# Softmax sums over keys by strided VectorE sums through DRAM, in a two-layer graph network on one core

## The chip, the core and the metric

The kernel runs on one core of one Trainium2 chip. The metric is the device time of one execution in microseconds (us). Before the change the median of three runs is 2721.17 us (2719.03 to 2722.04).

A core has five engines that run side by side, each with its own queue of instructions, executed in order: TensorE (PE, matrix products), VectorE (DVE), ScalarE (ACT), GpSimd (POOL) and SyncE (SP). In this kernel nearly all DMA transfers are issued by SP; 16 DMA engines carry them out. An instruction waits until the semaphores it needs are set, and everything behind it on the same engine waits with it.

## The reference

The input x is 64 batches of 256 tokens with 512 features, and adj is a 256 x 256 matrix of zeros and ones. Everything is float32. Layer 0 is attention with 8 heads of 64 features, masked by adj; layer 1 is a graph attention layer with one head. Each has a residual connection and a layer norm.

```python
# layer 0
q, k, v = x @ Wq + bq, x @ Wk + bk, x @ Wv + bv          # split into 8 heads
scores = einsum('bqhd,bkhd->bhqk', q, k) / sqrt(64) + (1 - adj) * -1e9
attn = softmax(scores, axis=-1)                          # sums over keys k
out = einsum('bhqk,bkhd->bqhd', attn, v)
x = layernorm(x + out @ Wo + bo)
# layer 1
h = x @ W
e = leaky_relu((h @ a1)[:, :, None] + (h @ a2)[:, None, :], 0.2) * adj
att = softmax(e, axis=2)
x = layernorm(x + elu(einsum('bij,bjf->bif', att, h) + beta * h))
```

The change concerns the denominators of the first softmax: for every batch, head and query, the sum of the exponentials over the 256 keys.

## The kernel before, in words

The kernel works on pairs of batches: 32 pairs, `pair(m, ...)`, each with two batches, `batch(m, s, ...)` with s 0 and 1.

For a pair, x is brought in transposed (`xin`, `xT`), and three products give q, k (features on partitions) and v (tokens on partitions). Each large product is done in two-by-two blocks with seven block products in place of eight (`project`, line 437 in the profile, tiles `ps_chain`, `ps_cross`, `ps_second`, `ps_fourth`, `ps_pair`). That needs sums and differences of the blocks of both sides. For Wq and Wk they are made once and stored in DRAM; in every later pair the seven left sides are fetched again, one at a time, into a rotating set of buffers called `piece` (`streamed`, lines 385 and 390). For Wv, Wo and W they stay in SBUF (`weight_sums`).

Attention of one batch (`attention_by_keys`): for each of four pairs of heads, TensorE makes the scores with keys on partitions and queries along the row (`scores`, line 756, tile `ps_sc`); VectorE adds the mask (line 763); ACT takes the exponential (line 765, tile `pT`, 128 partitions by two blocks of keys by 256 queries); POOL adds the two blocks of keys, so that 128 partial sums are left for every head and query (line 768, tile `both`). Then `denominators` sums over the 128 partitions by multiplying with ones on TensorE (line 781, tile `ps_den`), VectorE takes the reciprocal (line 798, tile `inv`), ACT sums both for a check of the range (line 794, into `range_sb`), and SP writes the rows of `inv` to DRAM and reads them back spread over all partitions (lines 806 and 810, tile `inv_all`). The values are mixed on TensorE without the denominators (`mixed`, line 733, tile `ps_pv`), copied out (line 831) and multiplied with `inv_all` by VectorE (line 836, tile `oT`). The product with Wo follows (`o`). The last batch takes its sums directly from `pT` and spreads the reciprocals with TensorE.

Layer 1 of a batch: two dot products with `wa_sb` (line 937), a row that is turned through DRAM (lines 960 to 963, tile `row`), `z` on VectorE (line 966), the leaky ReLU, mask, maximum, exponential and scale (lines 972 to 986, tile `e`), a transposition through DRAM (lines 1003 to 1010, `square`, `att_b`, `attT`), the product with x (`spread`, tile `yT`), the product with W (`u`), and the finish (lines 697 to 704).

The order of all instructions is fixed before the program is built. Every operation is entered in a `Plan` with its engine and an assumed duration. On TensorE the order is given by turns: `take_turn` sorts by round (the pair's number plus `LATER`) and, within a round, by the list `ROUND`; `FINISH` can give the operations of the last pairs an order of their own, and the last `OPEN` operations of TensorE may be placed in any order. `place` then lays the operations of all engines out in time with these durations, a lag between engines (`LAG`; for SP it stands for the transfer) and the numbers of buffers (`slots`), and what comes out is the order in every queue. Nothing of it is decided at run time.

## Time and profile before

| | |
|---|---|
| median of three runs | 2721.17 us |
| profiled execution | 2720.1 us |
| its span | 2718.3 us, granted TensorE clock 0.997 |
| TensorE busy | 2696.2 us, 99% |
| VectorE busy | 1956.4 us, 72% |
| ScalarE busy | 1548.9 us, 57% |
| GpSimd busy | 1721.8 us, 63% |
| DMA on SP's queue | 297.68 MB, 41.4% of 16 engines' span |

The profile comes from one execution. Its span runs from the first to the last instruction that the profiler saw; the execution's own time is 1.8 us longer. Busy time is the time in which an engine executed something, counted once where instructions overlap. Products of float32 show as two records each, so 8 of them show as 16. In the groups of instructions a row gives line, engine, operation, output and inputs, shapes and count; then the busy time, the mean time of one, the idle time of the engine before them and what ended it. For matrix products the mean of one is longer than what it occupies, since they overlap in a pipeline. In the list of waits a row gives who waited for whom, the total in us, the number of times and the longest.

### The profile page before, as it was taken

The page shows a single profiled execution, that of the slowest core. Times are in us where ns is not written, and L with a number is a line of the kernel's source. Part 1 is how long each engine was busy: PE and PEld are TensorE (multiplying, and loading weights), DVE is VectorE, ACT ScalarE, POOL GpSimd, SP SyncE. Part 2 cuts the span into 40 slices and gives each one's busy share as a digit, 9 for nine tenths or more (in the row PEclk, how much of TensorE's full clock was granted, in tenths as well). Part 3 has the DMA queues.
Part 4 walks back from the last instruction along what each step waited for, and adds up shares of the span by engine and source line. Part 5 has one row for each costly group of instructions (what it writes and reads, how often), then busy time and mean ns, then how long its engine had stood idle before and what let it go on. Part 6 is the DMA issues. An engine that isn't in the chain of part 4 may idle for free.

```text
span 2718.3 us, 47307 instructions
## 1 busy us (share of the span) xinstructions
PE 2696.2 (99%) x15919; PEld 2268.6 (83%) x15919; DVE 1956.4 (72%) x3677; ACT 1548.9 (57%) x3713; POOL 1721.8 (63%) x2254
## 2 busy tenths in 40 slices
PE   9999999999999999999999999999999999999997
PEld 7888888888888888888888888888888888888886
DVE  6777677777777677777767777777767777776766
ACT  3455556556556565565555655655656556555566
POOL 5756666665666656666666666566665666666654
PEclk9999999999999999999999999999999999999998
DMA  8434434344443444434443434444344443443221
GB/s 245 103 100 123 121 96 117 96 121 125 99 121 86 119 129 106 106 104 105 125 119 98 115 95 125 125 98 120 88 120 129 106 107 104 104 126 103 83 70 45
DMA packets 579056, 300.79 MB, mean 111 GB/s; under 512 B 404864, under 2 KB 509816, under 8 KB 578808
## 3 DMA queue, kind: packets, MB, share of 16 engines
q1 hardware_dynamic: 578680, 297.68, 41.4%
q8 instruction: 130, 2.13, 0.3%
q14 instruction: 118, 0.97, 0.1%
q0 software_dynamic: 128, 0.01, 0.0%
HBM read 245.11 MB, written 52.48 MB: 109 GB/s over the span
## 4 chain that ended last, share of the span: by engine, by line
PE 97%; DVE 1%; POOL 0%; ACT 0%; issue 0%; DMA 0%; SPq 0%; ACTq 0%; POOLq 0%; DVEq 0%
PE ps_chain L437 33%; PE ps_cross L437 22%; PE ps_pair L437 10%; PE ps_sc L756 8%; PE ps_pv L733 8%; PE ps_second L437 6%; PE ps_fourth L437 6%; PE ps_den L781 2%; DVE junk L543 0%; DMA xin<-in_x_dram 0%; ACT junk L569 0%; DMA row<-line 0%; SPq L631 0%; PE ps_y L1021 0%; PE ps_plain L502 0%
## 5 line engine op out<-in xcount | busy, mean ns | idle before, releaser
L768 POOL TENSOR_TENSOR both<-pT 128x256 f32<-128x256 f32 x504 | 354.6, 731 | 383.1 <-ACT pT L765 383.1
L763 DVE TENSOR_TENSOR pT<-ps_sc,maskT_sb 128x512 f32<-128x512 f32 x512 | 324.0, 680 | 85.4 <-PE ps_sc L756 85.4
L765 ACT ACTIVATE pT<-pT 128x512 f32<-128x512 f32 x512 | 304.0, 625 | 52.3 <-DVE pT L763 49.7
L937 DVE SCALAR_TENSOR_TENSOR junk<-x,wa_sb 128x512 f32<-128x512 f32 x256 | 206.8, 833 | 109.4 <-ACT x L586 108.2
L756 PE MATMUL ps_sc<-qT,kT 64*128 64x256 f32 x2048 | 238.4, 382 | 0.0
L733 PE MATMUL ps_pv<-pT,v 128*64 128x256 f32 x2048 | 235.1, 382 | 0.0
L756 PEld LDWEIGHTS ps_sc<-qT,kT 64*128 64x128 f32 x2048 | 192.8, 187 | 44.4 <-issue 24.6
L474 ACT COPY u<-ps_chain 128x256 f32<-128x256 f32 x126 | 46.9, 372 | 318.4 <-PE ps_chain L437 318.2
L586 ACT ACTIVATE x<-x,nmr,rs 128x512 f32<-128x512 f32 x256 | 197.5, 808 | 44.7 <-POOL nmr L582 44.6
L733 PEld LDWEIGHTS ps_pv<-pT,v 128*64 128x64 f32 x2048 | 141.4, 137 | 91.0 <-DVE kT L483 12.8
L1046 POOL TENSOR_TENSOR X_sums<-x 128x256 f32<-128x256 f32 x126 | 151.6, 1213 | 100.1 <-ACT x L586 98.6
L569 ACT ACTIVATE junk<-x,mean 128x512 f32<-128x512 f32 x256 | 182.2, 714 | 3.8 <-DVE mean L575 3.6
L569 ACT ACTIVATE junk<-x 128x512 f32<-128x512 f32 x256 | 159.4, 625 | 38.6 <-DVE x L914 31.8
L717 POOL TENSOR_TENSOR x<-x,res_sb 128x512 f32<-128x512 f32 x128 | 175.7, 1374 | 0.0
L580 POOL TENSOR_SCALAR rs<-sq 128x2 f32<-128x2 f32 (+1 forms) x130 | 34.8, 268 | 208.8 <-ACT junk L569 203.5
L408 POOL TENSOR_TENSOR oS<-oT 128x256 f32<-128x256 f32 x126 | 92.2, 731 | 86.7 <-DVE mean L575 53.0
L836 DVE TENSOR_TENSOR oT<-oT,inv_all 128x512 f32<-128x512 f32 x126 | 132.7, 1091 | 0.0
L975 POOL TENSOR_TENSOR e<-e,adj_sb 128x512 f32<-128x512 f32 (+1 forms) x66 | 82.2, 1247 | 77.0 <-DVE e L972 77.0
L437 PE MATMUL ps_chain<-so_sb,oS 128*128 128x256 f32 x504 | 129.3, 379 | 0.0
L437 PE MATMUL ps_chain<-sw_sb,yS 128*128 128x256 f32 x504 | 129.2, 379 | 0.0
L798 DVE RECIPROCAL inv<-ps_den 128x256 f32<-128x256 f32 x64 | 112.5, 1758 | 18.5 <-ACT junk L794 9.3
L408 POOL TENSOR_TENSOR yS<-yT 128x256 f32<-128x256 f32 x126 | 91.8, 729 | 51.7 <-DVE yT L483 31.8
(242 smaller groups left out, 7162.7 us busy)
## 6 DMA issues: line engine op xcount, KB each, us to landing
x<-in_x_dram SPq DMA_DIRECT2D x64, 512.0 KB
out_dram<-x SPq DMA_DIRECT2D x128, 256.0 KB
inv_all<-rows SPq DMA_DIRECT2D x126, 256.0 KB
xin<-in_x_dram SPq DMA_DIRECT2D x248, 128.0 KB
wq_sums<-wq_sums SPq DMA_DIRECT2D x124, 256.0 KB
wk_sums<-wk_sums SPq DMA_DIRECT2D x124, 256.0 KB
wq_sums<-in_L_gnn_Wq_dram SPq DMA_DIRECT2D x93, 256.0 KB
wk_sums<-in_L_gnn_Wk_dram SPq DMA_DIRECT2D x93, 256.0 KB
```

The source lines that it names most:

```text
L408: plan.op("POOL", 180 + 545 * width // P, lambda: nc.gpsimd.tensor_tensor(dst(), p(), m(), ALU.subtract), reads, writes)
L437: nc.tensor.matmul(dst[:, f, :], lhs, rhs, start=start and f == 0 and c == 0, stop=c == inner - 1, skip_group_check=True)
L569: plan.op("ACT", 700, lambda: nc.scalar.activation(junk[A], X[:, t, :], func, bias=mean[:, i:i + 1] if bias else 0.0, accum_out=to[:, i:i ...
L586: plan.op("ACT", 810, lambda i=i, t=t: nc.scalar.activation(X[:, t, :], X[:, t, :], AF.Identity, bias=nm[:, i:i + 1], scale=rs[:, i:i + 1] ...
L717: plan.op("POOL", 1270, lambda t=t: nc.gpsimd.tensor_tensor(X[:, t, :], X[:, t, :], res_sb[A], ALU.add), [res_sb], tokens(t))
L733: nc.tensor.matmul(acc[r * HD:(r + 1) * HD, i, :], V[:, 2 * k + s, h * HD:(h + 1) * HD], pT[h][:, k, :], start=k == 0, stop=k == NT - 1)
L756: nc.tensor.matmul(acc[j][:, k, :], kT[r:r + HD, c, key_blk(k)], own(qT, r, c), start=True, stop=True)
L763: plan.op("DVE", 690, lambda h=h, i=i: nc.vector.tensor_add(pT[h][A], acc[i][A], maskT_sb[A]), [acc[i], maskT_sb], [pT[h]])
L765: plan.op("ACT", 620, lambda h=h: nc.scalar.activation(pT[h][A], pT[h][A], AF.Exp, scale=1.0 / HD ** 0.5), [pT[h]], [pT[h]])
L768: plan.op("POOL", 725, lambda h=h, i=i: nc.gpsimd.tensor_tensor(both[c][:, i, :], pT[h][:, 0, :], pT[h][:, 1, :], ALU.add), [pT[h]], [(bot ...
L937: plan.op("DVE", 780, lambda t=t, i=i, junk=junk: nc.vector.scalar_tensor_tensor(junk[A], X[:, t, :], 1.0, wa_sb[:, i, :], op0=ALU.mult, o ...
L1046: plan.op("POOL", ns, lambda: nc.gpsimd.tensor_tensor(dst(), p(), m(), op), reads, writes)
```

## The change

The denominators of all batches but those of the last pair are no longer summed by TensorE. SP writes the four tiles `both` of a batch to DRAM (`keys`: 128 partial sums by 8 heads by 256 queries, 1 MB) and reads them back in four loads of another layout (`few`: in each group of 32 partitions, one partition holds 32 keys by 64 of the 2048 sums, in runs of 256 bytes). VectorE adds up the 32 keys in four strided sums (`part`). Four groups of keys are left; they go through DRAM once more (`parts`, `four`), and VectorE adds these and takes the reciprocal on 64 partitions by 32 columns (`den`). SP writes the reciprocals to `rows`, and the spread to `inv_all` is the same as before, now in a function of its own, `to_all`. The check of the range sums 32 columns on 64 partitions in place of 256 on 128; `range_sb` is set to one first. The last pair (`near`) takes its sums on TensorE directly from `pT`, as the last batch did before, in `denominators_near`.

With that go: the left sides of the product with Wv are streamed through `piece` like those of Wq and Wk, so that `wv_sb` and its sums no longer stay in SBUF, and there are seven `piece` buffers, not six; `z` is made by ACT, except in the last pair; `ROUND` has another order, `FINISH` is empty, `OPEN` is 60 and the lag of SP 5000 ns.

```diff
-ROUND = ("sums1", "mix1", "scores0", "spread1", "v", "u1", "attention0", "sums0", "mix0", "scores1", "o1", "x",
-         "logits1", "q", "spread0", "o0", "attention1", "u0", "k", "logits0")
+ROUND = ("sums1", "mix1", "scores0", "v", "spread1", "sums0", "mix0", "scores1", "attention0", "o1", "x", "k",
+         "logits1", "u1", "q", "spread0", "o0", "u0", "attention1", "logits0")
...
-FINISH = (("sums1", 1), ("mix1", 1), ("scores0", 0), ("v", 0), ("attention0", 1), ("spread1", 2), ("sums0", 0), ("u1",
...
+FINISH = ()
...
-    LAG = {"PE": 260.0, "DVE": 70.0, "ACT": 70.0, "POOL": 90.0, "SP": 4200.0}
+    LAG = {"PE": 260.0, "DVE": 70.0, "ACT": 70.0, "POOL": 90.0, "SP": 5000.0}
...
-    OPEN = 70
+    OPEN = 60
...
-    slots = {"xin": 2, "x": 4, "two": 6, "xP": 1, "piece": 6, "full": 4, "half": 18, "xS": 2, "st": 76, "ps": 8, "rows": 4, "svT": 4, "line": 4, "square": 4}
+    slots = {"xin": 2, "x": 4, "two": 6, "xP": 1, "piece": 7, "full": 4, "half": 18, "xS": 2, "st": 76, "ps": 8, "rows": 4, "svT": 4, "line": 4, "square": 4,
+             "keys": 3, "parts": 3, "few": 1, "part": 2, "four": 2, "den": 2}
...
-    wv_sb = weight(Wv, "wv_sb")
...
+    plan.op("POOL", 100, lambda: nc.gpsimd.memset(range_sb[A], 1.0), [], [range_sb])
...
-            wq_sb, wk_sb = sb("two", [C, D], "wq_sb"), sb("two", [C, D], "wk_sb")
+            wq_sb, wk_sb, wv_sb = (sb("two", [C, D], name) for name in ("wq_sb", "wk_sb", "wv_sb"))
...
+            load(wv_sb, Wv)
...
-            left["v"] = weight_sums(wv_sb, "sv_sb", "POOL")
+            lv, left["v"] = streamed(wv_sb, Wv, "wv_sums")
...
-        project(left["v"], right, False, [V], *gather(
-            lambda q: (lambda: V[:, 2 * q[1]:2 * q[1] + 2, half(q[0])], (V, q)), wide=True), width=N)
+        project(lv if m == 0 else left["v"], right, False, [V], *gather(
+            lambda q: (lambda: V[:, 2 * q[1]:2 * q[1] + 2, half(q[0])], (V, q)), wide=True), width=N, first=m == 0)
...
             def denominators():
+
+                keys, parts = Buf(dram_pool, "keys", [P, H * N], "keys"), Buf(dram_pool, "parts", [4, H * N], "parts")
+                for c in range(C):
+                    plan.op("SP", 500, lambda c=c: nc.sync.dma_start(
+                        keys[:, 2 * c * N:2 * (c + 1) * N], both[c][A].rearrange("p i n -> p (i n)")), [both[c]],
+                        [(keys, c)])
+
+                few, part = sb("few", [32, 64], "few"), sb("part", [64], "part")
+                for g in range(4):
+                    plan.op("SP", 800, lambda g=g: nc.sync.dma_start(
+                        few[32 * g:32 * g + 32], keys[32 * g:32 * g + 32, :].rearrange("k (c n) -> c k n", n=64)),
+                        [keys], [(few, g)])
+                for j in range(4):
+                    plan.op("DVE", 950, lambda at=slice(16 * j, 16 * j + 16): nc.vector.tensor_reduce(
+                        part[:, at], few[:, :, at].rearrange("p k n -> p n k"), AX.X, ALU.add), [few], [(part, j)])
+                plan.op("SP", 500, lambda: nc.sync.dma_start(
+                    parts[A].rearrange("g (c n) -> (g c) n", n=64), part[A]), [part], [parts])
+                four, den = sb("four", [4, 32], "four"), sb("den", [2, 32], "den")
+                plan.op("SP", 500, lambda: nc.sync.dma_start(
+                    four[0:HD], parts[A].rearrange("g (c n) -> c g n", n=32)), [parts], [four])
+                plan.op("DVE", 340, lambda: nc.vector.tensor_reduce(
+                    den[0:HD, 0, :], four[0:HD].rearrange("p g n -> p n g"), AX.X, ALU.add), [four], [(den, 0)])
+                plan.op("DVE", 280, lambda: nc.vector.reciprocal(den[0:HD, 1, :], den[0:HD, 0, :]), [(den, 0)],
+                        [(den, 1)])
+                for i in range(2):
+                    junk = sb("half", [32], "junk")
+                    plan.op("ACT", 400, lambda i=i, junk=junk: nc.scalar.activation(
+                        junk[0:HD], den[0:HD, i, :], AF.Identity, accum_out=range_sb[0:HD, i, b:b + 1]), [(den, i)],
+                        [junk, (range_sb, (i, b))])
+                plan.op("SP", 500, lambda: nc.sync.dma_start(
+                    rows[A].rearrange("h (c n) -> (h c) n", n=32), den[0:HD, 1, :]), [(den, 1)], [rows])
+                to_all()
+
+            def denominators_near():
                 turn("sums")
...
-                    for k in range(NT if last else 1):
+                    for k in range(NT):
...
-                                    pT[2 * c + i][:, k, :] if last else both[c][:, i, :],
...
-                if last:
-                    plan.op("PE", 1500, pe, pT, [acc], mode="sums", claims=[inv])
-                else:
-                    plan.op("PE", 1000, pe, both, [acc], mode="sums", claims=[inv])
...
+                plan.op("PE", 1860, pe, pT, [acc], mode="sums", claims=[inv])
                 plan.op("DVE", 1750, lambda: nc.vector.reciprocal(inv[A], acc[A]), [acc], [inv])
...
-            spread_inv = denominators()
+            spread_inv = denominators_near() if near else denominators()
...
         for t in range(NT):
-            plan.op("DVE", 480, lambda t=t: nc.vector.tensor_scalar(
-                z[:, t, :], row[A], sv[:, t, 1:2], None, ALU.add), [row, (sv, (0, t))], [(z, t)])
+            if near:
+                plan.op("DVE", 480, lambda t=t: nc.vector.tensor_scalar(
+                    z[:, t, :], row[A], sv[:, t, 1:2], None, ALU.add), [row, (sv, (0, t))], [(z, t)])
+            else:
+                plan.op("ACT", 440, lambda t=t: nc.scalar.activation(
+                    z[:, t, :], row[A], AF.Identity, bias=sv[:, t, 1:2]), [row, (sv, (0, t))], [(z, t)])
```

In both versions `both` is made for every batch whose sums do not come directly from `pT`: all but the last one before, all but the last two after.

## The prediction

> **What bounds the kernel now.** I read the page from the top: the span, the engines' busy time, then the chain that ended last, followed back from the last instruction.
>
> ```profile
> span 2718.3 us, 47307 instructions
> ...
> PE 2696.2 (99%) x15919; PEld 2268.6 (83%) x15919; DVE 1956.4 (72%) x3677; ACT 1548.9 (57%) x3713; POOL 1721.8 (63%) x2254
> ...
> PE 97%; DVE 1%; POOL 0%; ACT 0%; issue 0%; DMA 0%; SPq 0%; ACTq 0%; POOLq 0%; DVEq 0%
> ```
>
> TensorE is busy all the time and makes up 97% of the chain; no other engine reaches three quarters. Busy time by stretch (columns: stretch, its length, busy time of PE, PEld, DVE, ACT, POOL with instruction counts, granted clock, mean busy share of the 16 DMA engines, GB/s) shows one steady round of one pair of batches, then the start and the last pair:
>
> ```profile
> 1007.94:1091.58 83.64, 83.64 (x498) 70.61 (x498) 60.64 (x114) 48.27 (x116) 53.67 (x70) 1.00 0.44 111
> 8.00:90.00 82.00, 80.91 (x429) 67.95 (x428) 61.00 (x88) 30.78 (x68) 50.45 (x50) 1.00 0.81 222
> 2597.20:2718.30 121.10, 104.56 (x597) 83.88 (x597) 79.60 (x176) 72.68 (x175) 59.74 (x92) 0.94 0.19 56
> ```
>
> A round is 83.64 us with PE busy for all of it. DMA is light in the round (0.44) but heavy at the start (0.81). TensorE's own waits, the longest of them, are these; the first is the program's start, the next two lie in the last pair:
>
> ```profile
> PE tr_x L620 <- DMA xin<-in_x_dram: 4.3, 2, 3.7
> PE ps_chain L437 <- ACT attT L999: 1.5, 1, 1.5
> PE tr_a L996 <- DVE rc L983: 1.4, 1, 1.4
> ```
>
> So time taken off TensorE's queue counts in full, as long as nothing new makes it wait. The groups of the sums (busy, mean ns, then idle before) and one round's piece of TensorE's timeline (start, duration):
>
> ```profile
> L781 PE MATMUL ps_den<-both,ones 128*32 128x256 f32 x1008 | 67.5, 385 | 0.0
> L798 DVE RECIPROCAL inv<-ps_den 128x256 f32<-128x256 f32 x64 | 112.5, 1758 | 18.5 <-ACT junk L794 9.3 <-PE ps_den L781 9.2
> L966 DVE TENSOR_SCALAR z<-row,s 128x256 f32<-128x256 f32 x124 | 65.1, 566 | 6.9 <-DMA row<-line 6.4
> L977 DVE TENSOR_REDUCE nm<-e 128x2 f32<-128x512 f32 (+1 forms) x66 | 43.5, 659 | 2.0 <-POOL e L975 2.0
> ```
>
> ```profile
> 1085.09 1.89 PE L437 MATMUL ps_chain<-xS,wk_sums 128*128 128x256 f32 x8
> 1086.90 1.07 PE L781 MATMUL ps_den<-both,ones 128*32 128x256 f32 x16
> 1087.91 3.67 PE L733 MATMUL ps_pv<-pT,v 128*64 128x256 f32 x32
> ```
>
> The sums of one batch occupy 67.5/63 = 1.07 us of busy time, and 1.01 us from their start to the next group's start.
>
> [...]the store to square is issued at 1027.57 us and the reads that wait for it at 1029.66, 2.1 us. [...]The loads into few fill 32 partitions at a time, as those of att_b do[...]; the four sums step by 256 bytes, and no row of the kernel before shows such a step.
>
> **The change part by part**, against the profiled execution (2720.1 us, its span 2718.3; the median of the three timed runs is 2721.17, so 1.1 us above it).
>
> *Taken off TensorE.* 62 of 63 batches lose their ps_den group: 62 x 1.01 to 1.07 = 62.6 to 66.3 us. I take 64. Batch 62 goes from 8 to 16 products, which the last batch's group already shows (start to start 1.86 us against 1.01): +0.9.
>
> *VectorE, per batch.* Out: the reciprocal 1.76 and two z operations (2 x 0.53 = 1.05 by busy time): 2.8 us. In: four strided sums of 32 x 16 elements a partition. Nearest row L977, 128x512 in, 0.66 us contiguous; [...]I bound it above by double, 1.32; taken 1.0, so 4.0 (2.6 to 5.3). The two small operations on 64 partitions: I take 0.3 each. Net +1.8 (0.4 to 3.1), +3.6 a round: 60.6 + 3.6 = 64 of about 81.5 us, 79%. Free on the average; covered by TensorE's own work, and uncovered it would cost those 3.6 us a round, 112 over 31 rounds.
>
> *ACT.* z moves here: two 128x256 ACTIVATEs of about 0.44 (L794 0.41, L477 0.46), +0.9 per batch. The two range sums shrink from 256 columns to 32, between 0 and -0.8. At most +1.8 a round on 48.3. POOL: one memset more; its additions (L768, 0.73 us) stay.
>
> *SP's queue.* Before, 48 DMAs a pair: x 2, out 4, inv_all 4, xin 8, q and k pieces 14, square 2, att_b 8, line 2, row 2, rows 2. Added: keys 8, few 8, parts 2, four 2, v pieces 7: 75. Issue times from the trace (about 0.38 us for a plain one, 0.66 for one with 1024 pieces as xin, 0.6 for small ones): 8 x 0.38 + 8 x 0.66 + 4 x 0.6 + 7 x 0.36 = 13 us on some 24, 37 of 81.5. Room, but in order: while SP stands at few (waiting for keys to land) every piece and store behind it stands too.
>
> *DMA engines.* Prices from these stretches (same columns): the store to square with 256 KB, the four loads of att_b with 256 KB in 2048 packets, and a piece-rich stretch:
>
> ```profile
> 1028.00:1029.50 1.50, 1.50 (x9) 1.32 (x8) 0.67 (x2) 0.67 (x2) 1.42 (x2) 1.00 0.50 175
> 1030.50:1034.50 4.00, 4.00 (x34) 2.68 (x35) 1.52 (x4) 1.68 (x4) 3.31 (x3) 1.00 0.45 72
> 1050.50:1054.00 3.50, 3.50 (x18) 3.09 (x17) 2.11 (x4) 2.24 (x6) 2.92 (x4) 1.00 0.83 293
> ```
>
> Square: 0.50 x 1.5 = 0.75 us of all 16 engines, so keys (1 MB) 3.0 a batch. att_b: 0.45 x 4.0 = 1.8 us, 14 ns of one engine for each packet. few has 4096 packets of 256 bytes a batch: 3.6 us if a packet costs the same, 7.2 if a byte does; taken 5.4. Pieces: 0.83 x 3.5 = 2.9 us for 1.03 MB, 0.74 each, 5.2 for seven. A pair adds 6.0 + 10.8 + 5.2 + about 1 = 23 (19 to 27) to 0.44 x 83.64 = 36.8: 60 of 81.5 us, 73%. Hidden on the average.
>
> *The new chain of one batch.* After the last addition of both: keys 2.1, few about 7 (four issues, 5.4 of data[...]), sums 4, parts 2, four 2, small sums 1, rows 1.9 (issue at 1035.95, inv_all's at 1037.82), inv_all 3.7: 24 us. In the new order scores0 is followed by v 12.1, spread1 3.1, mix0 3.7, scores1 3.7, o1 6, k 12.1, u1 6, q 12.1, spread0 3.1, then o0 (durations of these groups in the trace): 62 us. The additions end 12.5 us after scores0 began (1007.9 to 1020.4), so about 25 us remain. sums1 is needed only in the next round's o1, later still. Not on the path.
>
> *v streamed.* With seven buffers the pieces of a product set can all be fetched before it begins; k and q follow each other with only u1's 6 us between, yet q's first piece may load as soon as k's first product is done, 18 us ahead. At the start four sums of Wv move from POOL to VectorE (wq_sums shows 1.64 us each, 6.6 in all, needed only behind scores0 at about 38 us), four stores of 256 KB are added, and the first keys and few fall where the DMA engines already run at 0.81: 82 x 0.81 = 66 us, plus about 20, is 86 of 82. I charge 4 us (0 to 12). If the engines had spare capacity there, it would be 0.
>
> *The end.* No order by FINISH, the last 60 TensorE operations free in place of 70, batch 62 without keys: the last pair's PE idle is 16.5 us; I charge +2 (-5 to +8).
>
> *Small waits.* DMA at 73% and VectorE at 79% will now and then be late: 0.15 us a round, 5 us (0 to 20).
>
> Sum: 2720.1 - 64 + 0.9 + 4 + 2 + 5 = **2668 us**, median taken the same. Its own range is 2650 to 2692.
>
> **Rivals.** *Partly eaten.* Pieces of q stand behind few and xin (1 MB, up to 3.2 us for one issue[...]), and each batch loses half to nine tenths of its microsecond: 2668 + 62 x (0.5 to 0.9) = 2699 to 2724, about 2705. For it: keys1, few1, xin and q's pieces all fall within k and u1. Against it: not one TensorE wait on a piece before.
>
> *VectorE stands at few: slower.* The four sums sit in order in VectorE's queue. If few lands late, behind them wait the additions that empty PSUM (L483, L914), and TensorE runs out of its eight PSUM buffers. The price is what TensorE stands per batch; it decides at 1.0 us, where the saving is gone. Assuming that few is 5 us late and that PSUM covers 3 of them, TensorE stands 2: 2668 + 124 = 2790. For it: order fixed beforehand, no slack in PE. Against it: the 25 us of slack let the sums be placed late, and VectorE stood only 6.4 us in 15 waits for row, its one regular DMA wait.
>
> *DMA becomes the bound.* few's packets would have to cost (83.6 - 36.8 - 12.2) x 16 / 8192 = 68 ns to cancel the gain, nearly five times att_b's. At 90 ns a round is 95 us, and the kernel near 3070. Only an effect of the 8 KB step between the rows of keys that att_b (1 KB step) doesn't show could do it.
>
> **How the numbers follow.** A change under 0.2% (5.4 us) can't be told from none. As forecast 0.58; partly eaten 0.14 (0.09 of it still faster, 0.05 no change); VectorE at few 0.20; DMA-bound 0.08. Faster 0.67, same 0.05, slower 0.28. The range 2648 to 2785 holds nearly all of the first two and half of the third, about 0.8.
>
> **What would show it.** Right: ps_den left in two batches only; a steady round of 81.5 us with PE busy throughout; DMA share near 0.73; the strided sums near 1.0 us each; PE still above 98%. Wrong: a round above 83.6 us; TensorE or VectorE waiting for few, wv_sums, wq_sums or wk_sums; DMA share near 1; a sum of 1.5 us or more; over 12 us lost before 100 us or after the last pair began.

## The result and the profile after

The changed kernel takes 2740.09 us (median of five runs, 2734.37 to 2744.66) against 2720.3 us before (median of five on the same chip, the three above among them): 1.0073 of it, 95% interval 1.0058 to 1.0089. It is 0.7% slower, where 1.9% faster was forecast. The profiled execution takes 2742.66 us, its span is 2740.9 us, 22.6 us more than before.

The page of the kernel after: span, busy times, SP's DMA queue (packets, MB, share of 16 engines), and the shares of the chain that ended last.

```profile
span 2740.9 us, 47862 instructions
...
PE 2662.1 (97%) x14943; PEld 2253.8 (82%) x14943; DVE 2026.7 (74%) x3867; ACT 1567.8 (57%) x3837; POOL 1627.3 (59%) x2243
...
q1 hardware_dynamic: 945800, 489.76, 72.1%
...
PE 78%; DVE 9%; DMA 7%; issue 2%; ACT 1%; SPq 1%; POOL 0%; DVEq 0%; ACTq 0%; POOLq 0%
```

TensorE has lost its 976 records (61 x 16: 62 groups gone, one made longer) and 34 us of busy time, yet the span grew. The chain tells why: 97% of it was TensorE, now 78%, and 16% is VectorE and DMA together. Busy time by stretch of the kernel after (columns as before: a round, the start, the last pair):

```profile
1361.84:1444.92 83.08, 82.12 (x466) 69.93 (x464) 61.80 (x121) 48.60 (x119) 50.36 (x70) 1.00 0.76 186
8.00:90.00 82.00, 72.31 (x357) 59.76 (x356) 51.30 (x80) 25.63 (x55) 35.33 (x35) 0.96 0.91 247
2609.93:2740.90 130.97, 106.95 (x615) 85.55 (x613) 85.99 (x185) 77.22 (x189) 58.22 (x93) 0.93 0.18 56
```

A round is shorter, but by 0.6 us and not by 2; TensorE now stands for 0.96 us in it. In the same 82 us of the start it does 8.6 us less work, and the last pair takes 131 us. TensorE's waits (total, times, longest):

```profile
PE ps_pair L435 <- DVE yT L481: 16.5, 27, 0.9
PE ps_chain L435 <- ACT yT L472: 11.8, 6, 4.6
PE ps_pair L435 <- DVE x L942: 8.0, 27, 0.3
PE ps_chain L435 <- DVE oT L864: 6.1, 1, 6.1
...
PE ps_b L523 <- DVE pT L762: 4.4, 1, 4.4
PE ps_chain L435 <- ACT v L472: 4.2, 1, 4.2
```

Two waits come back in 27 places, about once a round; the long single ones lie at the start. To read all runs alike, I divide a span into the start (up to scores0 of the third pair), 29 rounds from there to scores0 of the last pair, and the end. All these times are read from TensorE's timeline.

| us | start | one round | end | span |
|---|---|---|---|---|
| before | 170.8 | 83.66 | 121.2 | 2718.3 |
| after | 195.5 | 83.26 | 131.0 | 2740.9 |
| difference | +24.7 | 29 x -0.407 = -11.8 | +9.8 | +22.6 |

Without the two groups of sums (1.00 us each) and with nothing else, a round would be 81.66 us. So of 58 us taken out of the rounds, 46 came back, and start and end cost 34 more. Start, round and end are read from one profiled execution each. A measure of their spread: two runs below that differ only in the order of the end (e_few_wide and c_wide_finish) differ by 2.7 us in the start and by 0.13 us in a round.

**Where a round loses it.** Group by group, in the mean of the 29 rounds, every stretch of TensorE's timeline has its old length to within 0.2 us but two: spread0, 4.12 us in place of 3.15, and o0, 6.55 in place of 6.05. The groups of VectorE concerned (busy, mean ns, then idle before):

```profile
L795 DVE TENSOR_REDUCE part<-few 128x16 f32<-128x512 f32 x248 | 243.8, 1034 | 14.3 <-DMA few<-keys 14.3
L864 DVE TENSOR_TENSOR oT<-oT,inv_all 128x512 f32<-128x512 f32 x126 | 96.7, 805 | 40.0 <-DMA inv_all<-rows 40.0
```

The sums cost what was forecast. VectorE stands 40 us for `inv_all`, at the multiplication L864, in 26 places. One round of the timeline of the kernel after (start, duration), the chain of one batch's sums and what stands behind it; the lines between these are left out:

```profile
1376.36 1.68 SPq L785 DMA_DIRECT2D keys<-both  x2
1382.22 3.76 SPq L791 DMA_DIRECT2D few<-keys  x4
1392.44 3.90 DVE L795 TENSOR_REDUCE part<-few 128x16 f32<-128x512 f32 x4
1396.76 0.42 SPq L797 DMA_DIRECT2D parts<-part  x1
1402.64 0.62 SPq L800 DMA_DIRECT2D four<-parts  x1
1410.47 0.92 SPq L811 DMA_DIRECT2D rows<-den  x1
1416.86 1.29 SPq L776 DMA_DIRECT2D inv_all<-rows  x2
1423.71 1.29 DVE L864 TENSOR_TENSOR oT<-oT,inv_all 128x512 f32<-128x512 f32 x2 [1.48 <-DMA inv_all<-rows]
1427.07 0.42 DVE L481 TENSOR_TENSOR yT<-ps_pair,yT 128x256 f32<-128x256 f32 x1
1427.63 0.68 PE L435 MATMUL ps_pair<-att_sums,x 128*128 128x128 f32 x4 [0.66 <-DVE yT L481]
1431.06 1.84 DVE L1018 SCALAR_TENSOR_TENSOR e<-e,rc,diag_sb 128x256 f32<-128x256 f32 x2
```

From the last keys issued to the multiplication are 45.7 us. VectorE stands 1.48 us for `inv_all`; behind it in the queue are the additions that empty q's and yT's PSUM buffers, and TensorE, ready for `ps_pair`, stands 0.66 us for one of them. A little later o0 stands for `x` L942, which is queued behind the two `e` L1018 of 1.84 us.

**The start.** Windows from scores0 of the first pair to its scores1, and on to scores0 of the second pair, before and then after:

```profile
33.99:54.53 20.54, 20.54 (x137) 16.19 (x136) 13.56 (x24) 8.59 (x17) 10.26 (x13) 1.00 0.85 253
54.53:96.37 41.84, 40.74 (x232) 33.27 (x230) 32.17 (x52) 17.19 (x40) 34.12 (x36) 1.00 0.63 158
```

```profile
35.23:62.31 27.08, 21.75 (x122) 16.84 (x121) 16.08 (x33) 7.63 (x13) 10.54 (x11) 0.94 0.92 273
62.31:116.23 53.92, 43.27 (x216) 34.83 (x214) 27.40 (x44) 15.33 (x39) 30.05 (x30) 0.91 0.87 182
```

18.6 us are lost in these two stretches. TensorE stands 5 and 11 us in them, and its granted clock is lower (0.94, 0.91), so it is slow as well as idle. The records of the clock show where: it is at 0.50 for 3.4 or 6.8 us about the end of each long stall, and at 1.00 otherwise. The first products after the stall of 4.19 us take twice their time:

```profile
49.93 3.66 PE L435 MATMUL ps_chain<-wv_sums_s,xS 128*128 128x256 f32 x8 [4.19 <-ACT v L472]
53.43 1.89 PE L435 MATMUL ps_fourth<-wv_sb,xS 128*128 128x256 f32 x8
```

The waits in the two stretches are the single ones above: v's product waits for `v` L472; `ps_b` stands 4.4 us for `pT`, as VectorE has stood 5.9 us for the first `few`; o0 stands 6.1 us for `oT`, as VectorE has stood 7.3 us for the second `few`. The other 6 us of the start come before these stretches (1.2 us) and in the second pair, where TensorE stands 4.6 us for `yT` L472.

### The profile page after: what moved, and what is told of

Read it like the earlier page. It is cut to its first block, busy times and chain, and to the rows that moved or that the text cites. A ratio compares the mean times of both kernels' runs of the same rounds, so it can differ in the third digit from the quotient of the medians.

```text
span 2740.9 us, 47862 instructions
## 1 busy us (share of the span) xinstructions
PE 2662.1 (97%) x14943; PEld 2253.8 (82%) x14943; DVE 2026.7 (74%) x3867; ACT 1567.8 (57%) x3837; POOL 1627.3 (59%) x2243
## 4 chain that ended last, share of the span: by engine, by line
PE 78%; DVE 9%; DMA 7%; issue 2%; ACT 1%; SPq 1%; POOL 0%; DVEq 0%; ACTq 0%; POOLq 0%
PE ps_chain L435 27%; PE ps_cross L435 17%; PE ps_pair L435 9%; PE ps_sc L755 8%; PE ps_pv L732 8%; DMA inv_all<-rows 6%; PE ps_second L435 4%; PE ps_fourth L435 4%; DVE e L1018 2%; DVE oT L864 1%; DVE x L697 1%; DVE part L795 1%; DVE qT L481 1%; DVE x L942 1%; ACT junk L567 1%
## 5 line engine op out<-in xcount | busy, mean ns | idle before, releaser
L764 ACT ACTIVATE pT<-pT 128x512 f32<-128x512 f32 x512 | 290.8, 621 | 90.4 <-DVE pT L762 90.4
L1078 POOL TENSOR_TENSOR X_sums<-x 128x256 f32<-128x256 f32 x126 | 98.8, 784 | 317.8 <-PE ps_cross L435 180.8
L795 DVE TENSOR_REDUCE part<-few 128x16 f32<-128x512 f32 x248 | 243.8, 1034 | 14.3 <-DMA few<-keys 14.3
L716 POOL TENSOR_TENSOR x<-x,res_sb 128x512 f32<-128x512 f32 x128 | 160.6, 1276 | 141.9 <-ACT u L472 69.1
L965 DVE SCALAR_TENSOR_TENSOR junk<-x,wa_sb 128x512 f32<-128x512 f32 x256 | 186.2, 746 | 50.6 <-ACT x L584 48.4
L732 PEld LDWEIGHTS ps_pv<-pT,v 128*64 128x64 f32 x2048 | 141.3, 137 | 80.0 <-issue 11.8
L406 POOL TENSOR_TENSOR oS<-oT 128x256 f32<-128x256 f32 x126 | 105.3, 835 | 67.4 <-DVE oT L864 45.2
L1078 POOL TENSOR_TENSOR att_sums<-attT 128x128 f32<-128x128 f32 x126 | 72.6, 576 | 113.9 <-DVE attT L1042 109.1
L859 ACT COPY oT<-ps_pv 128x512 f32<-128x512 f32 x128 | 73.9, 577 | 102.1 <-PE ps_pv L732 102.1
L435 PE MATMUL ps_chain<-so_sb,oS 128*128 128x256 f32 x504 | 129.4, 379 | 0.0
L864 DVE TENSOR_TENSOR oT<-oT,inv_all 128x512 f32<-128x512 f32 x126 | 96.7, 805 | 40.0 <-DMA inv_all<-rows 40.0
L475 ACT ACTIVATE kT<-ps_chain,bk_sb 128x256 f32<-128x256 f32 x128 | 53.6, 470 | 123.2 <-PE ps_chain L435 123.1
```

The lines of the kernel that those rows point to most:

```text
L435: nc.tensor.matmul(dst[:, f, :], lhs, rhs, start=start and f == 0 and c == 0, stop=c == inner - 1, skip_group_check=True)
L716: plan.op("POOL", 1270, lambda t=t: nc.gpsimd.tensor_tensor(X[:, t, :], X[:, t, :], res_sb[A], ALU.add), [res_sb], tokens(t))
L732: nc.tensor.matmul(acc[r * HD:(r + 1) * HD, i, :], V[:, 2 * k + s, h * HD:(h + 1) * HD], pT[h][:, k, :], start=k == 0, stop=k == NT - 1)
L764: plan.op("ACT", 620, lambda h=h: nc.scalar.activation(pT[h][A], pT[h][A], AF.Exp, scale=1.0 / HD ** 0.5), [pT[h]], [pT[h]])
L795: plan.op("DVE", 950, lambda at=slice(16 * j, 16 * j + 16): nc.vector.tensor_reduce(part[:, at], few[:, :, at].rearrange("p k n -> p n k") ...
L965: plan.op("DVE", 780, lambda t=t, i=i, junk=junk: nc.vector.scalar_tensor_tensor(junk[A], X[:, t, :], 1.0, wa_sb[:, i, :], op0=ALU.mult, o ...
```

## The experiments

Each was run beside the kernel before, whose median was 2719.9 to 2720.8 us each time; ratios are against it, with 95% intervals. e_no_wait, e_short_sums and e_few_quarter leave out part of the work, as their texts say; the others do all of it. All runs at a glance:

| run | time us | ratio | start | round | end |
|---|---|---|---|---|---|
| after | 2740.1 | 1.0073 [1.0058, 1.0089] | 195.5 | 83.26 | 131.0 |
| e_tensor_sums | 2740.8 | 1.0077 [1.0060, 1.0094] | 178.4 | 83.65 | 134.3 |
| e_no_wait | 2730.3 | 1.0036 [1.0023, 1.0049] | 197.2 | 82.68 | 132.9 |
| e_end_order | 2725.3 | 1.0020 [1.0013, 1.0027] | 171.3 | 83.65 | 125.7 |
| e_v_streamed | 2729.7 | 1.0034 [1.0021, 1.0046] | 181.7 | 83.65 | 121.5 |
| e_short_sums | 2728.5 | 1.0030 [1.0019, 1.0042] | 192.7 | 82.88 | 130.9 |
| e_few_quarter | 2710.0 | 0.9955 [0.9939, 0.9972] | 185.0 | 82.52 | 130.2 |
| e_hops | 2780.7 | 1.0221 [1.0193, 1.0250] | 188.3 | 84.69 | 136.0 |
| c_mend | 2771.0 | 1.0186 [1.0169, 1.0203] | 189.5 | 84.62 | 126.1 |
| e_few_512 | 2839.5 | 1.0436 [1.0417, 1.0456] | 202.5 | 86.65 | 130.1 |
| c_512f | 2828.6 | 1.0409 [1.0391, 1.0428] | 203.5 | 86.15 | 123.4 |
| e_few_wide | 2725.9 | 1.0021 [1.0014, 1.0027] | 192.3 | 82.91 | 130.6 |
| e_512_wide | 2754.8 | 1.0112 [1.0098, 1.0125] | 195.3 | 83.78 | 129.4 |
| c_512_wide | 2741.0 | 1.0073 [1.0060, 1.0086] | 193.9 | 83.75 | 122.7 |
| c_wide_finish | 2718.9 | 0.9995 [0.9986, 1.0003] | 195.0 | 82.78 | 123.6 |
| c_wide_early | 2717.7 | 0.9988 [0.9979, 0.9996] | 176.2 | 83.31 | 123.8 |
| c_best | 2700.3 | 0.9934 [0.9920, 0.9947] | 175.3 | 82.66 | 124.4 |

### Is it the wait, or what came with it?

**e_no_wait**: the changed kernel, the multiplication takes another operand of the same shape.

```diff
-oT[:, part, :], oT[:, part, :], everywhere[:, part, :]
+oT[:, part, :], oT[:, part, :], everywhere[:, part, :] if near else adj_sb[A]
```

> The changed kernel, with the same instructions in the same order on every engine, except that the multiplication of oT reads adj_sb in place of inv_all (not in the last pair): the output is not scaled by the reciprocals. All transfers stay. Theory W (VectorE stands at this multiplication until inv_all lands, and the additions behind it keep TensorE waiting): spread0 falls from 4.12 to about 3.15 us, o0 from 6.55 to 6.05, 29 rounds give back some 43 us, the two waits of 6.2 and 4.6 us at the start with their slow restarts some 13 more: about 2685 us. Theory L (VectorE and the DMA engines are merely busier): within 10 us of the changed kernel's 2740.

The round falls by 0.58 us to 82.68, 17 us over 29 rounds; start and end are each about 2 us longer. TensorE's two waits that came back once a round are now these:

```profile
PE ps_pair L435 <- DVE x L942: 8.2, 27, 0.3
...
PE ps_pair L435 <- DVE yT L481: 1.2, 3, 0.7
```

The one for `yT` is all but gone (16.5 us in 27 places before), and spread0 falls from 4.12 to 3.30 us; the next scores0 lengthens by 0.26 us in the mean, in ten of the 29 rounds, which leaves 0.58. So the wait for `inv_all` explains most of what spread0 lost, and 0.58 of the 1.6 us that a round lost. It does not explain o0, which keeps its 6.55. The time, 2730, is where theory L put it and far from W's 2685: W had the mechanism of spread0, but not of o0 and the start.

**e_tensor_sums**: everything of the change but the sums themselves, which go back to TensorE.

```diff
-            def denominators(): ...
-                    for k in range(NT):
+                    for k in range(NT if near else 1):
-                                    pT[2 * c + i][:, k, :]
+                                    pT[2 * c + i][:, k, :] if near else both[c][:, i, :]
-            spread_inv = denominators_near() if near else denominators()
+            spread_inv = denominators_near()
```

> The changed kernel with the sums back on TensorE (as before the change: both, ps_den, reciprocal of 256 columns), all else as changed: v streamed, z on ACT, the new order, no FINISH. Theory W: the steady round returns to 83.64 us without stalls; the start keeps what v streamed and the new order cost, some 13 us, and loses the two waits for oT; the end keeps 10: about 2743 us. If the whole loss at the start comes from keys and few on the DMA engines: about 2730. If v streamed itself stalls TensorE in each round: above 2760.

It takes as long as the changed kernel, and near theory W's 2743, though not in its parts: the start keeps 7.6 us of its loss where 13 were expected, the end 13 where 10 were. What came with the sums (v streamed, the new order, the end) costs some 21 us by itself; the sums by VectorE on top of it gain 11.4 us in the rounds and 3.3 at the end, and lose 17.1 at the start: about nothing. o0 is 6.05 us here, so its half microsecond comes with VectorE's new sums and the order that the plan gives with them.

**e_end_order** and **e_v_streamed**: the kernel before, with one of these parts alone.

```diff
-FINISH = (("sums1", 1), ...
+FINISH = ()
-    OPEN = 70
+    OPEN = 60
```

> The kernel before, with FINISH empty and OPEN 60, nothing else. If the order of the last pairs is what made the end longer (130.9 us after the last scores0 in place of 121.1): about 2730 us. If the end was longer through the sums and transfers: 2720.

The time, 2725, lies between both expectations: the end grows by 4.5 us and nothing else moves. The new end is 9.8 us longer, so the order of the last stretch is nearly half of it.

```diff
-    wv_sb = weight(Wv, "wv_sb")
-            left["v"] = weight_sums(wv_sb, "sv_sb", "POOL")
+            load(wv_sb, Wv)
+            lv, left["v"] = streamed(wv_sb, Wv, "wv_sums")
-"piece": 6
+"piece": 7
```

> The kernel before, with v's left sides streamed through seven piece buffers, nothing else. If the streaming costs the start its time (four sums of Wv on VectorE, 1 MB more to store, a first product of v that waits): 2725 to 2733 us, all of it before 120 us. If the start's loss comes from the new order and the sums' transfers: 2719 to 2723. A stall in each round (DMA share about 0.5) would show as a round above 83.64: not expected by either.

As the first expectation had it, the start is 10.9 us longer, and the rounds don't feel it. TensorE's longest waits in this run:

```profile
PE ps_chain L436 <- ACT v L473: 6.8, 1, 6.8
PE tr_x L619 <- DMA xin<-in_x_dram: 4.8, 2, 3.5
```

The second is the program's start, as before. The first is v's product. In VectorE's queue the last additions of `pT` come behind layer 1's constants (L542), which wait 2.4 us for W, and in ACT's queue the copies of v's first blocks come behind the exponentials of these `pT`. A reason for this order may be that v's four sums hold four of the 18 `half` buffers while they are stored; that was not shown (see c_mend).

### What makes the sums late?

**e_short_sums** adds 4 keys in place of 32, **e_few_quarter** reads 8 in place of 32 and adds them four times over, so that VectorE works as long as in the changed kernel.

```diff
-few[:, :, at].rearrange("p k n -> p n k")
+few[:, 0:4, at].rearrange("p k n -> p n k")
```

> The changed kernel, same instructions and order; each strided sum adds 4 of its 32 keys only, so that VectorE is occupied about 0.2 us in place of 1.03 (3.3 us less per batch); the sums are partial. All transfers stay. If VectorE's load is what makes o0 (0.5 us a round) and the start late: o0 back to 6.05, spread0 near 3.2, a round of 81.8 us, and about 2740 - 29 x 1.4 = 2700. If it is the transfers' lateness alone: the chain ends 3.3 us earlier, spread0 gains at most 0.8 a round (as with the wait removed), o0 stays at 6.55, the start stays near 195: about 2715.

```diff
-few[32 * g:32 * g + 32], keys[32 * g:32 * g + 32, :]
+few[32 * g:32 * g + 32, 0:8, :], keys[32 * g:32 * g + 8, :]
```

> The changed kernel, same instructions and order; each of the four loads into few brings 8 of its 32 rows of keys (a quarter of the packets), and the sums read those 8 four times over, so that VectorE adds as many elements; the sums are partial. If the DMA engines' load through few is what makes inv_all late and the start long: DMA share 0.64 in place of 0.72, scores0 of the third pair at about 182 us in place of 195.5, spread0 near 3.3: about 2700. If the lateness is set by the order of the queue and its hops: within 8 us of 2740.

The short sums take 0.25 us each, 3.1 us less per batch, and a round gains 0.38; the time, 2728, misses both theories (2700 and 2715). The chain doesn't become shorter by them, as one round shows:

```profile
1382.12 3.51 SPq L785 DMA_DIRECT2D keys<-both  x3
1382.42 0.77 DVE L795 TENSOR_REDUCE part<-few 128x16 f32<-128x64 f32 x4
1386.74 0.42 SPq L797 DMA_DIRECT2D parts<-part  x1
```

The sums are done at 1383.19, but the store of `parts` stands in SP's queue behind three stores of `keys` of the other batch, and goes 3.6 us later. For the first batch of a pair `parts` goes 35.5 us after the start of its scores in the mean, against 35.0 in the changed kernel.

The smaller traffic of e_few_quarter gains 0.74 a round and 10.5 us at the start, with VectorE's work unchanged; 2710 is nearest to the theory of the traffic (2700). Its DMA queue, and what VectorE still stands for `inv_all` (40.0 us in the changed kernel):

```profile
q1 hardware_dynamic: 755336, 441.00, 60.0%
```

```profile
  DMA inv_all<-rows: 4.6, 5
```

So with a quarter of `few`'s traffic `inv_all` is hardly ever late. The chain as a whole is only 1.0 us shorter, though (49.0 against 50.0, table below): for the batch that VectorE stands for, everything up to the small sum stands where it stood, 47.0 us after the start of its scores, and only `rows` and `inv_all` are issued sooner, by 0.8 and 1.4 us. The difference of the shares also prices `few`: (0.721 x 2740.9 - 0.600 x 2708.3) / 0.75 / 62 = 7.55 us of all 16 engines a batch. That counts what `few` adds to the other packets too, since those are shorter in e_few_quarter (those of 2 KB take 100.9 ns in place of 103.4). By the records of its own packets, sorted by size, one of `few` takes 23.6 ns of one engine in the changed kernel, 6.0 us of all 16 a batch.

**e_hops** and **c_mend**: the planner is told 3.0 us for keys, 3.5 for parts and four and 2.5 for rows (in place of 5.0) and asks for `inv_all` only once `oT` is there; c_mend adds the old `FINISH` and puts v's four sums into `piece` buffers.

```diff
+    def op(..., lag=None)          # keys 3000, parts and four 3500, rows 2500
-    plan.op("SP", 1000, spread, [rows], [(everywhere, i)])
+    plan.op("SP", 1000, spread, [rows, (oT, 0)], [(everywhere, i)])
```

> The changed kernel with shorter assumed lags for four kinds of transfers of the chain (keys 3.0 us, parts and four 3.5, rows 2.5, in place of 5.0; nothing else in the plan changes but that inv_all may not be loaded before oT is there), which moves these transfers and the work behind them forward in every queue. All work is done. If inv_all is late because each hop is placed 5 us after the one before: inv_all lands some 6 us earlier, spread0 falls to about 3.2 us and the start to about 185: about 2700. If the transfers themselves need that long: no gain, or new waits of VectorE for four and of SP for den: 2735 to 2760.

> As the one with the shorter hops, and besides the four sums of Wv are kept at the start in piece buffers, not in half (which the first scores need), and FINISH is that of the kernel before. All work is done. If the three losses are what the profile says (start 25 us, of which 11 through v's streaming; rounds 46 us; end 10, of which 4.5 through the order): start 178 to 183, a round of 82.0 to 82.6, an end of 125: 2685 to 2705, faster than both. If the hops don't help: about 2722.

Both lose, more than any theory had it: the round goes to 84.7 and 84.6 us. Not where the changed kernel lost it: o0 is back at 6.05 us, but u0 takes 8.4 us in place of 6.2. With less time planned, VectorE meets the small transfers before they land: in e_hops it stands 88.9 us for `four`, in 27 places, up to 4.2 us. So planning less time does not make the chain early enough. c_mend's end is 126.1 us. Its start is no shorter than that of e_hops (189.5 against 188.3 us), so that other buffers for v's four sums did not cure the start by themselves.

### Fewer packets, or other partitions?

**e_few_512** loads `few` in runs of 512 bytes, 8 transfers on 16 partitions each, half the packets (the sums, `parts` and `four` follow: eight groups of 16 keys); **c_512f** adds the old `FINISH`.

```diff
-few[32 * g:32 * g + 32], keys[32 * g:32 * g + 32, :].rearrange("k (c n) -> c k n", n=64)
+few[16 * i:16 * i + 16], keys[16 * i:16 * i + 16, :].rearrange("k (c n) -> c k n", n=128)
```

> The changed kernel with few's transfers in runs of 512 bytes: 8 groups of 16 partitions, each with 16 keys of 128 columns, so that few has 2,048 packets a batch in the place of 4,096; the same bytes, the same order of all work, all of it done. Theory A (the small transfers are late because few's packets keep the DMA engines busy): the share of the queue of SP falls from 72% to about 58 to 66%, VectorE's wait for inv_all falls from 40 us to under 20, the round from 83.26 to about 82.7 us and the start (to the third pair's scores0) from 195 to about 187; the time is 2712 to 2728 us. Theory B (it is the bytes, or the chain of waits itself, that sets the lateness; not the number of packets): the share, the wait and the round stay within 0.15 us of the changed kernel's and the time within 0.3% of 2740 us.

> The same as the run with runs of 512 bytes, and the order of the last stretch (FINISH) of the kernel before put back; all work done. Theory A (few's packets and the end's order are two separate costs): the end, from the last pair's scores0, falls from about 131 to about 126 us, so that this run is 4 to 6 us below the one without FINISH, 2707 to 2723 us, and at or below the kernel before. Theory B (the end is set by the late sums of the last batch, not by its order): the end stays at 130 us or more and the two runs agree within 2 us.

Neither theory holds for the time: half the packets made it 3.6% slower than the changed kernel, and the queue's share rose. (The old `FINISH` does shorten the end, to 123.4 us.)

```profile
q1 hardware_dynamic: 838664, 493.84, 75.9%
```

The slow transfers hold up others too: VectorE now stands 67.2 us for the transposition of layer 1 (`attT`), against 2.3 us in the changed kernel.

```profile
DVE attT L1043 <- DMA att_b<-square: 67.2, 28, 5.4
```

By the same reckoning `few` now takes 7.55 + (0.759 x 2845.3 - 0.721 x 2740.9) / 62 = 10.5 us a batch (the larger `parts` and `four`, and what is added to other packets, included); one of its packets takes 59.0 ns, 7.6 us a batch in place of 6.0. What had changed beside the run's length was the number of transfers and of the partitions that one transfer fills. The next three runs change only the partitions (and the order of the rows in `parts` with them).

**e_few_wide** (the changed kernel, runs of 256 bytes), **e_512_wide** (e_few_512), **c_512_wide** (that with the old `FINISH`):

```diff
-few[32 * g:32 * g + 32], keys[32 * g:32 * g + 32, :]
+few[g:P:4], keys[32 * g:32 * g + 32, :]
-parts[A].rearrange("g (c n) -> (g c) n", n=64)
+parts[A].rearrange("g (c n) -> c g n", n=64)
```

> The changed kernel, with each of the four transfers of few landing on every fourth partition (g, g+4, ..., all 128 partitions reached by four of 32 each) in the place of 32 neighbouring ones; the same packets of 256 bytes, bytes, order and work. Theory P (the partitions that a transfer reaches set its rate): the share of the queue of SP falls from 72% to 66% or less, VectorE's wait for inv_all from 40 us to under 20, the round from 83.26 to under 82.9 us; 2715 to 2730 us. Theory Q (the count of packets, or their length, sets it; the partitions do not matter): share 71 to 73%, round 83.1 to 83.4 us, time within 0.2% of 2740 us.

> The run with runs of 512 bytes (2839 us), with each of its eight transfers landing on every eighth partition in the place of 16 neighbouring ones; nothing else differs. Theory P (its loss came of the 16 neighbouring partitions): the share of the queue of SP falls from 75.9% to 58 to 66%, the round from 86.65 to 82.4 to 82.9 us; 2705 to 2725 us. Theory Q (its loss came of the longer runs or of the eight transfers in the place of four): share and round stay above 74% and 85.5 us, time above 2810 us.

> The same as the run with runs of 512 bytes on every eighth partition, with the order of the last stretch (FINISH) of the kernel before put back; all work done. Theory P with a separate cost of the end's order: 4 to 8 us below that run, 2700 to 2718 us, so at or below the kernel before (2720 us). Theory Q: within 12 us of 2829 us.

The queue of e_few_wide: same packets, same bytes.

```profile
q1 hardware_dynamic: 945800, 489.76, 68.6%
```

14 us less than the changed kernel by the partitions alone; VectorE's wait for `inv_all` falls from 40 to 17 us. The share falls less than expected (68.6%, not 66%), the round comes to the edge of what was expected (82.91). The two runs with 512 bytes end between both theories. For the 512-byte runs the same step is worth 85 us and ten points of share (75.9 to 65.9%), but they stay behind e_few_wide.

| `few` lands on | run of | one packet | own packets a batch | by the difference of shares |
|---|---|---|---|---|
| 32 neighbouring partitions | 256 bytes | 23.6 ns | 6.0 us | 7.55 us |
| every fourth of 128 | 256 bytes | 19.1 ns | 4.9 us | 5.85 us |
| 16 neighbouring partitions | 512 bytes | 59.0 ns | 7.6 us | 10.5 us |
| every eighth of 128, in pairs | 512 bytes | 28.7 ns | 3.7 us | 4.95 us |

For each length of run the wider spread is the cheaper one, 19.1 ns a packet in place of 23.6 and 28.7 in place of 59.0; why was not shown.

But a lower share is not an earlier end: e_512_wide has a lower share than e_few_wide and a longer round. Among the runs that keep the changed kernel's plan, the round goes with the chain's length, from the end of the last keys' issue to the multiplication, averaged over the 46 or 47 batches between 300 and 2300 us:

| run | chain us | round us |
|---|---|---|
| e_few_quarter | 49.0 | 82.52 |
| c_wide_finish | 49.2 | 82.78 |
| e_few_wide | 49.3 | 82.91 |
| e_short_sums | 49.7 | 82.88 |
| after | 50.0 | 83.26 |
| e_512_wide | 50.5 | 83.78 |
| e_few_512 | 52.4 | 86.65 |

A microsecond of the chain is about one of the round here. That is no proof that the chain sets the round: the chain also grows when TensorE stands, as its steps stand in queues between work that TensorE paces, and in e_few_512 part of the round is the wait for `attT`. e_hops does not fit: a chain of 48.1 us with a round of 84.69. In e_512_wide the eight issues of `few` take 8.2 us from first to last, in e_few_wide the four take 6.3; the last is followed sooner by its sum, but the chain ends 1.1 us later. In SP's queue issues of the other batch's `few` stand between `four` and `inv_all`, so that the number of issues can be the reason (the planner was told the time of one issue for two of them); it was not tried by itself.

### Putting start and end right

**c_wide_finish** is e_few_wide with the old `FINISH`. **c_wide_early** leaves the first pair's sums on TensorE, puts v's four sums in `piece` buffers, layer 1's constants behind u0, and tells the planner 5.5, 5.5 and 4.5 us for parts, four and rows; **c_best** tells it 4.8, 4.8 and 4.0.

```diff
+        early = m is not None and m < 1 and not general
-            spread_inv = denominators_near() if near else denominators()
+            spread_inv = denominators_near() if near or early else denominators()
-        S = {n: sb("half", [2, F], f"{name}_s{n}") for n in (1, 2, 3, 4)}
+        S = {n: sb("piece" if name == "wv_sums" else "half", [2, F], f"{name}_s{n}") for n in (1, 2, 3, 4)}
-            plan.turn = (0, ROUND.index("k"))
+            plan.turn = (0, ROUND.index("u0"))
```

> The run with few on every fourth partition (2725.9 us), with the order of the last stretch (FINISH) of the kernel before put back; all work done. Theory A (the end's order costs what it cost the kernel before, 4.5 us, or what c_512_wide gained by it, 6.7 us): the end falls from 130.6 to 124 to 126 us, start and round stay at 192 and 82.9; 2719 to 2722 us, level with the kernel before. Theory B (the end is held by the late sums): it stays at 130 us, time 2724 to 2728.

> The same, with the first pair's sums over keys left to TensorE as in the kernel before, the four sums of v's streamed left side put in buffers of pieces in the place of half buffers, layer 1's constants placed at u0 in the place of k, and the planner told 5.5, 5.5 and 4.5 us as the time from the issue of parts, four and rows to the next step (these latencies were measured at 5.9, 5.3 and 4.3 us; LAG gives 5.0 to all); all work done. Theory A (the start's 21 us over the kernel before are the first pair's waits for few and the half buffers that v's sums hold): the start falls from 192 to 175 to 180 us, the round stays at 82.9 to 83.3, the end at 121 to 125; 2706 to 2722 us. Theory B (the start's loss lies in the traffic of the first 80 us): the start stays at 186 us or more and the time at 2722 us or more.

> The run with the first pair's sums on TensorE and few on every fourth partition (2717.7 us), with the planner told 4.8, 4.8 and 4.0 us for parts, four and rows in the place of 5.5, 5.5 and 4.5; nothing else differs, all work done. That run lost per round 0.5 us more than c_wide_finish (83.31 against 82.78 us), 40 us of it waits for inv_all. Theory A (the order of the small transfers against the other work sets the round, so that start and round can be had together): start 174 to 178, round 82.7 to 83.0, end 121 to 125; 2697 to 2709 us. Theory B (with the start cured the round stays above 83.2 us whatever the order): 2712 us or more.

The old order gives back 7.0 us of the end (130.6 to 123.6), and with it the kernel is level with the one before. All three runs came out within 1 us of what their theory A had for the time, c_wide_early at the upper edge of its round. The early parts give back 16 to 20 us of the start, but that is three edits together and other planned times, so which of them counts most is open (c_mend had one of them alone, the buffers, without gain). c_wide_early loses its gain in the rounds again: 83.31 us, VectorE standing 40.4 us for `inv_all`. c_best changes only the planned times against c_wide_early, keeps the start, and its round of 82.66 us is as short as that of c_wide_finish (82.78). Its page:

```profile
span 2696.8 us, 47699 instructions
...
PE 2651.7 (98%) x14975; PEld 2256.1 (84%) x14975; DVE 2001.3 (74%) x3857; ACT 1568.1 (58%) x3837; POOL 1638.4 (61%) x2243
...
PE 87%; DMA 4%; DVE 4%; issue 2%; ACT 2%; SPq 1%; POOL 1%; DVEq 0%; ACTq 0%; POOLq 0%
```

It beats both kernels: 0.66% faster than before and 40 us faster than the changed one. Against before: start +4.5, rounds 29 x -1.00 = -29.1, end +3.2, together -21.4 us of span. TensorE is 87% of the chain, not 97: spread0 still takes 4.01 us in place of 3.15.

## Why the prediction was wrong

**What held.** The sums leave TensorE at 1.00 us each (64 us forecast for 62). A strided sum takes 1.034 us (taken 1.0); VectorE has 61.8 us in a round (64 forecast), the DMA engines 76% of the round shown (73%). The pieces of v, k and q are never late in a round (its products keep 12.1 us). So "partly eaten", where q's pieces were to be late, has a nearer time (2705) by luck and the wrong cause; "DMA becomes the bound" is out. That 2740 lies inside the range of 2648 to 2785 is owed to the rivals that the range was widened for, not to the sum.

**The step that failed: the new chain of one batch, 24 us with 25 to spare.** Measured against its terms (means in the kernel after, and in e_hops, where the plan asks for everything sooner):

| step | predicted | after | e_hops |
|---|---|---|---|
| last keys issued to first few issue | 2.1 | 5.8 | 3.6 |
| few, first issue to first sum | 7 | 11.8 | 11.3 |
| the four sums, with what is queued between | 4 | 6.0 | 4.3 |
| end of the last sum to parts issued | 0 | 1.1 | 3.0 |
| parts issued to four issued | 2 | 5.9 | 4.8 |
| four issued to small sum | 2 | 4.8 | 2.8 |
| small sums, to rows issued | 1 | 1.2 | 1.6 |
| rows issued to inv_all issued | 1.9 | 4.3 | 5.0 |
| inv_all issued to multiplication | 3.7 | 7.8 | 10.3 |
| all, with the issues of four and rows themselves | 24 | 50.0 | 48.1 |

The two microseconds for a transfer came from a round with DMA at 44% (2.1 us for square), and were laid end to end, as if every next step were at the head of its queue. They are not, and that could be read in the kernel before, in the round that the prediction used and at the beginning of the next: here is the same step for the two batches of a pair.

```profile
1035.95 0.64 SPq L806 DMA_DIRECT2D rows<-inv  x1
1037.82 1.30 SPq L810 DMA_DIRECT2D inv_all<-rows  x2
...
1090.36 0.62 SPq L806 DMA_DIRECT2D rows<-inv  x1
...
1098.61 1.33 SPq L810 DMA_DIRECT2D inv_all<-rows  x2
```

The prediction took the 1.9 us of the first; the second takes 8.2. From the issue of `rows` to the multiplication the kernel before needs 13.5 us for one batch and 14.1 for the other, with the DMA engines at 44%, and the changed kernel 13.1 and 12.3; the prediction has 5.6 for these two steps. So the chain is long mainly because each step stands in its queue behind other work, by the order that the plan fixed, and less by the load: with the share at 60% (e_few_quarter) it is still 49.0 us, and sums that are done 3 us earlier do not make it shorter (e_short_sums). The time of the transfer itself is part of it, and varies. Where VectorE does stand for `four`, its sum begins 4.6 us after the issue began in the changed kernel (16 places), 5.3 in e_few_quarter (5) and 2.6 in e_hops (27); what makes this difference stays open. In e_hops the steps up to the issue of `rows` shrink by 5 us together, but the last two, which e_hops also ties to `oT`, grow by 3, so that the whole chain shrinks by 1.9. At 50 us in place of 24 the chain uses up the slack. In the round shown the last keys are issued 16 us after scores0 began, the multiplication comes at 62 us and o0 at 67, and in VectorE's queue the multiplication stands ahead of additions that TensorE waits for.

**The rival "VectorE stands at few"** had that mechanism and the right side: VectorE held at a transfer, PSUM not emptied, TensorE waiting. But in the rounds the transfer is `inv_all`, not `few` (in the whole program four waits for `few`, 14.3 us, two of them, 13.2 us, at the start, where this rival does hold), and its price in a round is 0.6 us (e_no_wait), not 4.

**Small waits**, 5 us (0 to 20), measured 46 in the rounds: 0.97 us a round in spread0, 0.50 in o0, 0.1 elsewhere. The o0 part is no wait for a transfer: it stays in e_no_wait, e_short_sums and e_few_quarter, which have the changed kernel's order, and is all but gone in e_tensor_sums (6.05), e_hops (6.05) and c_best (6.10), whose orders differ. The trace puts it on `x` L942 behind `e` L1018; that was not tried alone, so its cause stays open.

**DMA engines, few 5.4 us a batch (3.6 to 7.2).** Its own packets take 6.0 us, inside the range; with what they add to others it is 7.55. The text took the price of att_b, which fills 32 partitions as well: 14 ns a packet of 128 bytes there, 23.6 for one of 256 here. Spread over every fourth partition `few` takes 4.9.

**The start, +4 (0 to 12): +24.7.** v streamed alone is +10.9, where the text saw VectorE's extra 6.6 us but not the constants of layer 1 ahead in VectorE's queue; the trace puts most of the rest on the waits for the first two `few`s and the lower clock after them. A quarter of `few`'s traffic gives 10.5 us back, and the edits of c_best 20.

**The end, +2 (-5 to +8): +9.8.** The order is 4.5 of it in the kernel before, 7.0 in c_wide_finish. What the rest is (2.8 to 5.3) stays open; e_tensor_sums, without any late sums, has it too.

In the sum -64 was right; +12 for everything else should have been +87 (22.6 + 64). Of these 87, 17 are shown to be the late `inv_all` (e_no_wait), 10.9 v streamed and 4.5 the order of the end, each tried alone. The 14.5 of o0 and about half of the end stay open; for the rest there are the waits in the trace, and e_few_quarter for 10.5 us at the start.

## What to carry to other kernels

Work that leaves the bound engine through DRAM is priced by its chain of round trips: count the steps, and take for each the spacing that the queues' order gives, for every batch of a pair, and not the shortest transfer in the trace. Here it was 4 to 6 us a step in place of 2. Then look at what stands behind the last step on its engine, since an in-order queue turns a late operand of one tile into a stall of another: in the round shown VectorE stood 1.48 us for `inv_all`, and TensorE 0.66 us for an addition behind it. Where transfers have short runs, try the spread of their partitions before cutting their packets: here the same packets on every fourth partition gave 14 us, and longer runs on 16 neighbouring ones cost 100. And when a change brings other orders along, measure them without it: here they cost as much as the change could have given.

## What was not expected of the hardware

Half the packets with the same bytes made a transfer slower when it filled 16 partitions in place of 32: 59.0 ns for a packet of 512 bytes against 23.6 for one of 256, 7.6 us a batch against 6.0. Spread over every eighth partition the same packet took 28.7 ns, and 85 us of the kernel came back.

TensorE's granted clock was 0.94 and 0.91 in stretches in which it stood for a fifth of the time, against 1.00 in the same stretches before. In the changed kernel it is at 0.50 for 3.4 or 6.8 us about the end of each of the five stalls of 4.2 to 6.1 us, so that such a stall cost more than its length: after the one of 4.19 us eight products took 3.66 us, the next eight 1.89. In the traces of all 18 kernels each of the 42 stalls of 4 us or more (after the first 10 us) has that, and only 6 of the 111 stalls between 1 and 2 us do; those of a round, 1.2 us at most in the changed kernel, left the clock at 1.00. Why it does so was not tried.
